# At most three sample gathers in flight in a deformable-convolution and mixture-of-experts kernel

## The chip, the core and the metric

The kernel runs on one core of one Trainium2 chip. The metric is the device time of one execution in microseconds (us); the time of a kernel is the median of its runs. The core has five engines that run their own instruction streams: TensorE (PE in the profile; its weight loads are listed as PEld), VectorE (DVE), ScalarE (ACT), GpSimd (POOL) and SyncE (SP). DMAs are issued by GpSimd and SyncE here, each through a queue of its own, and move data on the core's 16 DMA engines.

## The reference

The input `x` is 4 images of 256 channels and 64 x 64 pixels, in float32. First comes a residual branch: a normalisation over the channels and three modulated deformable 3 x 3 convolutions, each followed by a ReLU:

```
om   = conv3x3(x, w_off) + b_off              # 27 channels: 9 x (dy, dx) and 9 masks
ys   = gy + base_y + dy ;  xs = gx + base_x + dx
sampled = bilinear(x, ys, xs) * sigmoid(mask) # 9 samples of 256 channels for each pixel
out  = einsum('bikhw,oik->bohw', sampled, w) + b
```

A bilinear sample mixes four neighbouring pixels; outside the image they are zero. The branch's result is added to `x`. Then every pixel is a token of 256 features: a second residual branch normalises it, picks the two likeliest of 8 experts from a softmax gate, and adds the experts' outputs, weighted by their probabilities. An expert is 256 to 512, GELU, 512 to 256.

## The kernel before

**Stages and blocks.** A stage is one convolution layer of one image; `run` lists the 12 of them in `self.stages`, images interleaved so that the next layer of one image can be prepared beside another image's. A stage has 8 blocks of 512 pixels (`NB`, `BLK`), a block has 4 groups of 128 pixels (`TPB`) and 9 taps (`K`). `main_block` runs over the taps and, for each, over pairs of pixel groups: 36 gathers for a block, 288 for a stage, 3456 in all.

**The tables.** Each layer's input lies in HBM as a table (`tab`) in which a row holds a pixel's 256 channels and those of the pixel below it, so that two neighbouring rows, 4 KB, hold the four corners of a sample. `enter` writes the table through SyncE's queue. The offsets' convolution (line 357) and some VectorE work give, for each block, the row numbers `idx` and the mixing coefficients `cf`.

**One sample group.** `samples` issues an indirect DMA from GpSimd (line 503): 128 rows of 4 KB, 512 KB in all, into a buffer `g` of 128 x 1024 elements. VectorE then mixes the upper and lower corners (line 509) and the left and right ones (line 514), which gives `s`, 128 x 256, and ends the use of `g`. ScalarE multiplies with the mask (line 517). `turn`, which runs two pairs behind (`LAG = 2`), transposes a pair of samples on TensorE (line 532), ScalarE copies the result to SBUF (line 535), and when a tap's four groups are there `finish` multiplies the tap before it with its weights (line 555: four products of 128 x 128 by 128 x 512 into `acc`).

**Buffers and queues.** There are 10 buffers `g` (`GB = 10`) and 8 buffers `s`, so that VectorE can be some way ahead of TensorE. A gather waits until VectorE's line 514 has let go of the buffer that it takes. The DMAs of GpSimd's queue share eight landing semaphores in turn, so a DMA also waits until the eighth one in front of it on that queue has landed.

**The work beside it.** Around the gathers, in the same streams, stand the expert layers: for each of 163 expert steps `fetch` issues from GpSimd one weight gather (line 800, 128 rows of 9.2 KB) and two token gathers (line 812, 128 x 256); TensorE does lines 840, 856 and 874. `combine_fetch` (line 915) gathers the experts' results back, 256 times. A planner (`Lane`, `pump`) puts these pieces between the taps at a pace for each image. They begin when the first image has its third layer, after 2250 us, and are densest towards the end, where the last image's layers run beside them. GpSimd's queue is served in order: what stands behind a waiting gather waits with it.

Of the kernel before, what the change touches and what calls it, by code (L numbers as in the profile page):

```python
# [35 lines left out]
FT = 1 << FT_LOG  # L36
FU = FT // P
GB = 10
LAG = 2
LEAST = 2.0**-30  # L40
WINN = CC * (RPB + 2) * W
# [41 lines left out]
class Group:  # L83


    def __init__(self, b, n0, n1):
        self.b, self.n0, self.n1 = b, n0, n1
        self.nm = f"{b}_{n0}"
        self.M = (n1 - n0) * TPB

        self.NF = 2 * self.M * P // FT + E - 1


        self.half = (self.NF + 1) // 2
        self.zt, self.acc, self.gy, self.sums, self.py = {}, [], [], [], None
        self.order = [s // 2 + s % 2 * self.half for s in range(self.NF)]
# [21 lines left out]
class Weave:  # L118
# [3 lines left out]
    def __init__(self, ctx, tc, ins, out):  # L122
        nc = self.nc = tc.nc
        self.tc = tc
        self.ins = ins
        self.x = ins["x"].rearrange("b (c p) h w -> b p c (h w)", p=P)
        self.out_v = out.rearrange("b (c p) h w -> b p c (h w)", p=P)
        self.B = self.x.shape[0]

        def pool(name, bufs, **kw):  # L130
            return ctx.enter_context(tc.tile_pool(name=name, bufs=bufs, **kw))

        self.cst = pool("cst", 1)
        self.dram = pool("dram", 1, space=bass.MemoryType.DRAM)
        self.wkp = pool("wkp", 1)
        self.plan = pool("plan", 19)
        self.win = pool("win", 3)
        self.wt = pool("wt", 2)
        self.small = pool("small", 1)
        self.big = pool("big", 2)  # L140
        self.ffn = pool("ffn", 2)
        self.rt = pool("rt", 1)
        self.rt2 = pool("rt2", 2)
        self.gyp = pool("gyp", 4)
        self.smT = pool("smT", 2)
        self.smp = pool("smp", 8)
        self.gat = pool("gat", GB)
        self.ps = pool("ps", 3, space=bass.MemoryType.PSUM)
        self.ps1 = pool("ps1", 1, space=bass.MemoryType.PSUM)

        self.routes, self.tiles, self.sums = Lane(), Lane(), Lane()
        self.side, self.plans_side = [], []
        self.last = self.gathered = self.turned = None
        self.starting, self.draining, self.later = True, False, []
        self.pend, self.pairs = None, []

# [323 lines left out]
    def main_block(self, i, n, wins):  # L482
        l, b = self.stages[i]
        plan = self.plans.pop((l, b, n))
        for k in range(K):
            for t0 in range(0, TPB, 2):
                ss = self.samples(i, n, k, t0, plan)
                self.pairs.append((i, n, k, t0, wins, ss))
                if len(self.pairs) > LAG:
                    self.turn()  # L490
# [3 lines left out]
    def samples(self, i, n, k, t0, plan):  # L494


        nc = self.nc
        idx, cf = plan
        ss = []
        for t in (t0, t0 + 1):  # L500
            j = t * K + k
            g = self.gat.tile([P, 2, 2, C], F32, tag="g", name=f"g_{i}_{n}_{j}")
            self.gathered = nc.gpsimd.indirect_dma_start(  # L503
                out=g.rearrange("p x s f -> p (x s f)"),
                out_offset=None,
                in_=self.table(*self.stages[i]),
                in_offset=bass.IndirectOffsetOnAxis(ap=idx[:, j : j + 1], axis=0),
            )
            nc.vector.scalar_tensor_tensor(  # L509
                g[:, :, 0, :], g[:, :, 1, :], cf[:, j, 0:1], g[:, :, 0, :],  # L510
                ALU.mult, ALU.add,
            )
            s = self.smp.tile([P, C], F32, tag="s", name=f"s_{i}_{n}_{j}")
            self.last = nc.vector.scalar_tensor_tensor(  # L514
                s, g[:, 1, 0, :], cf[:, j, 1:2], g[:, 0, 0, :], ALU.mult, ALU.add
            )
            nc.scalar.activation(s, s, AF.Copy, scale=cf[:, j, 2:3])  # L517
            ss.append(s)
        return ss

    def turn(self):


        nc = self.nc
        i, n, k, t0, wins, ss = self.pairs.pop(0)
        nm = f"{i}_{n}_{k}"
        if t0 == 0:
            self.sT = self.smT.tile([P, CC, BLK], F32, tag="sT", name=f"sT_{nm}")
        tp = self.ps.tile([P, CC, 2 * P], F32, tag="tp", name=f"tp_{nm}_{t0}")
        for u in range(2):  # L530
            for c in range(CC):
                self.turned = nc.tensor.transpose(  # L532
                    tp[:, c, u * P : (u + 1) * P], ss[u][:, c * P : (c + 1) * P], self.ident
                )
        nc.scalar.copy(self.sT[:, :, t0 * P : (t0 + 2) * P], tp)  # L535
        if t0 + 2 == TPB:

            self.finish()
            self.pend = (i, n, k, self.sT, wins)
# [596 lines left out]
```

## Time and profile before

| | |
|---|---|
| median of 9 runs | 7514.78 us (7485.77 to 7528.69) |
| the profiled execution's own time | 7461.21 us |
| its span, first to last instruction | 7459.5 us |
| mean granted TensorE clock | 0.951 of full speed |
| bytes moved by DMA | 2223.73 MB, 298 GB/s on average |
| of these by GpSimd's queue (q0) | 1947.35 MB |
| gathers of line 503 | 3456, the first at 91.2 us, the last at 7007.0 us |
| GpSimd's time for one (writing its descriptors) | 939 / 975 / 3837 ns at least / median / at most |

Times in the profile count from the start of the span. An engine's busy time leaves out instructions that only wait or issue. A row of the timeline gives the start, the time taken, the engine, line and operation, and in brackets the idle time of the engine before it with what ended the wait; "issue" there means that the profile shows nothing that was waited for. For a GpSimd DMA the time taken is that of writing the descriptors; the data land later.

### The profile page before, as it was taken

The page shows a single profiled execution, that of the slowest core. Times are in us where ns is not written, and L with a number is a line of the kernel's source. Part 1 is how long each engine was busy: PE and PEld are TensorE (multiplying, and loading weights), DVE is VectorE, ACT ScalarE, POOL GpSimd, SP SyncE. Part 2 cuts the span into 40 slices and gives each one's busy share as a digit, 9 for nine tenths or more (in the row PEclk, how much of TensorE's full clock was granted, in tenths as well). Part 3 has the DMA queues.
Part 4 walks back from the last instruction along what each step waited for, and adds up shares of the span by engine and source line. Part 5 has one row for each costly group of instructions (what it writes and reads, how often), then busy time and mean ns, then how long its engine had stood idle before and what let it go on. Part 6 is the DMA issues. An engine that isn't in the chain of part 4 may idle for free.

```text
span 7459.5 us, 88985 instructions
## 1 busy us (share of the span) xinstructions
PE 6405.5 (86%) x26500; PEld 3594.1 (48%) x26500; DVE 4949.7 (66%) x11467; ACT 3263.0 (44%) x7141; POOL 4473.4 (60%) x4245
## 2 busy tenths in 40 slices
PE   7898888888898888889997888888888799978887
PEld 3443433334454444445554444444544455644665
DVE  6776777778997666667777656656768554667421
ACT  3444544445554444445453444444444343444322
POOL 4654666656666656556557656655656665666543
PEclk8999999999999999999998989999999999999988
DMA  8998999999999888888888888888888787888644
GB/s 270 338 326 277 355 339 339 350 339 354 365 355 320 303 303 297 291 316 320 316 309 302 300 278 316 303 294 297 316 306 299 253 275 248 289 303 289 212 139 124
DMA packets 800319, 2223.73 MB, mean 298 GB/s; under 512 B 104728, under 2 KB 302872, under 8 KB 794080
## 3 DMA queue, kind: packets, MB, share of 16 engines
q0 software_dynamic: 551200, 1947.35, 73.7%
q1 hardware_dynamic: 248640, 270.69, 10.9%
q8 instruction: 215, 3.52, 0.2%
q14 instruction: 264, 2.16, 0.1%
HBM read 2160.68 MB, written 196.40 MB: 316 GB/s over the span
## 4 chain that ended last, share of the span: by engine, by line
PE 68%; ACT 10%; issue 7%; another core or an unknown queue 6%; DVE 5%; DMA 2%; POOL 1%; SPq 0%; ACTq 0%; POOLq 0%; DVEq 0%
PE acc L555 34%; PE tp L532 10%; PE ph L856 7%; PE py L874 6%; PE po L357 6%; ACT sT L535 4%; ACT s L517 3%; DVE g L509 2%; DVE s L514 1%; PE pm L371 1%; ACT hT L866 1%; PE lp_tok L618 1%; PE ftp L840 1%; ACT win L577 1%
## 5 line engine op out<-in xcount | busy, mean ns | idle before, releaser
L503 POOL DMA_INDIRECT g<-tab,idx x3456 | 3686.0, 1067 | 2331.1 <-DVE s L514 1025.4
L555 PE MATMUL acc<-sT,wk 128*128 128x512 f32 x6912 | 3484.2, 619 | 259.5 <-ACT sT L535 151.2
L509 DVE SCALAR_TENSOR_TENSOR g<-g,cf 128x512 f32<-128x512 f32 x3456 | 2556.7, 742 | 262.4 <-DMA g<-tab,idx 246.6
L514 DVE SCALAR_TENSOR_TENSOR s<-g,cf 128x256 f32<-128x256 f32 x3456 | 1660.6, 482 | 1293.7 <-PE tp L532 701.1
L535 ACT COPY sT<-tp 128x512 f32<-128x512 f32 x1728 | 1002.1, 585 | 2303.3 <-PE tp L532 1534.0
L517 ACT ACTIVATE s<-s,cf 128x256 f32<-128x256 f32 x3456 | 1628.5, 508 | 241.3 <-DVE s L514 155.0
L555 PEld LDWEIGHTS acc<-sT,wk 128*128 128x128 f32 x6912 | 1193.0, 197 | 1110.5 <-issue 815.7
L532 PEld LDWEIGHTS tp<-ident,s 128*128 128x128 f32 x6912 | 889.7, 145 | 1640.9 <-issue 921.0
L532 PE MATMUL tp<-ident,s 128*128 128x128 f32 x6912 | 1278.0, 285 | 422.0 <-ACT s L517 220.9
L874 PE MATMUL py<-w,hT 128*128 128x256 f32 x2608 | 673.1, 396 | 109.5 <-ACT hT L866 64.0
L856 PE MATMUL ph<-fzT,w 128*128 128x256 f32 x2608 | 697.4, 401 | 64.1 <-ACT fzT L844 27.6
L874 PEld LDWEIGHTS py<-w,hT 128*128 128x128 f32 x2608 | 482.7, 195 | 250.8 <-ACT hT L866 100.9
L856 PEld LDWEIGHTS ph<-fzT,w 128*128 128x128 f32 x2608 | 492.4, 200 | 196.4 <-issue 67.4
L866 ACT ACTIVATE hT<-ph,w 128x256 f32<-128x256 f32 x652 | 281.9, 471 | 603.7 <-PE ph L856 353.8
L812 POOL DMA_INDIRECT zt<-z,tok x326 | 333.4, 1023 | 163.8 <-issue 88.3
L800 POOL DMA_INDIRECT w<-in_W,wrow x163 | 177.5, 1089 | 365.2 <-issue 126.7
L357 PE MATMUL po<-win,wo 128*32 128x504 f32 (+1 forms) x2304 | 365.0, 610 | 6.4 <-ACT win L301 2.1
L892 DVE TENSOR_TENSOR y<-py,w 128x512 f32<-128x512 f32 x163 | 111.7, 686 | 337.6 <-PE py L874 277.0
L915 POOL DMA_INDIRECT gy<-ys,slots x256 | 252.8, 988 | 105.0 <-issue 71.8
L930 DVE SCALAR_TENSOR_TENSOR ta<-gy,cw,ta 128x256 f32<-128x256 f32 x256 | 120.4, 479 | 127.2 <-DMA gy<-ys,slots 76.0
L357 PE MATMUL po<-win_pre,wo 128*32 128x504 f32 (+1 forms) x1152 | 184.9, 620 | 2.0 <-ACT om L366 2.0
L366 ACT ACTIVATE om<-po,bo 128x512 f32<-128x512 f32 x96 | 66.0, 687 | 257.4 <-PE po L357 164.5
(154 smaller groups left out, 2958.0 us busy)
## 6 DMA issues: line engine op xcount, KB each, us to landing
tab<-hv SPq DMA_DIRECT2D x512, 128.0 KB
g<-tab,idx POOLq DMA_INDIRECT x3456
ys<-y SPq DMA_DIRECT2D x163, 256.0 KB
tab<-h_pre SPq DMA_DIRECT2D x128, 256.0 KB
wk<-in_conv_w SPq DMA_DIRECT2D x99, 256.0 KB
xc_pre<-in_x SPq DMA_DIRECT2D x32, 512.0 KB
xr_tok<-in_x SPq DMA_DIRECT2D x32, 512.0 KB
t<-t_tok SPq DMA_DIRECT2D x32, 512.0 KB
```

Source lines behind the costliest of these rows:

```text
L357: nc.tensor.matmul(po[g * Q : (g + 1) * Q, :].rearrange("q (r w) -> q r w", w=W)[:, :, x0:x1], lhsT=self.wo[l][:, 3 * ky + kx, c, :], rhs= ...
L503: self.gathered = nc.gpsimd.indirect_dma_start(out=g.rearrange("p x s f -> p (x s f)"), out_offset=None, in_=self.table(*self.stages[i]), ...
L509: nc.vector.scalar_tensor_tensor(g[:, :, 0, :], g[:, :, 1, :], cf[:, j, 0:1], g[:, :, 0, :], ALU.mult, ALU.add,)
L514: self.last = nc.vector.scalar_tensor_tensor(s, g[:, 1, 0, :], cf[:, j, 1:2], g[:, 0, 0, :], ALU.mult, ALU.add)
L517: nc.scalar.activation(s, s, AF.Copy, scale=cf[:, j, 2:3])
L532: self.turned = nc.tensor.transpose(tp[:, c, u * P : (u + 1) * P], ss[u][:, c * P : (c + 1) * P], self.ident)
L535: nc.scalar.copy(self.sT[:, :, t0 * P : (t0 + 2) * P], tp)
L555: nc.tensor.matmul(acc[:, o, :], lhsT=self.wk[k][:, c, o * P : (o + 1) * P], rhs=sT[:, c, :], start=(k == 0 and c == 0), stop=(k == K - 1 ...
L812: self.nc.gpsimd.indirect_dma_start(out=zt, out_offset=None, in_=grp.zd, in_offset=bass.IndirectOffsetOnAxis(ap=grp.tok[:, j : j + 1], axi ...
L856: nc.tensor.matmul(ph[:, h, :], lhsT=w1[:, o : o + P], rhs=zT[:, c, :], start=(c == 0), stop=(c == CC - 1),)
L866: nc.scalar.activation(ht[:, h, :], ph[:, h, :], AF.Gelu, bias=w1[:, k : k + 1])
L874: nc.tensor.matmul(py[:, u, :], lhsT=hT[h // 2][:, h % 2, u * P : (u + 1) * P], rhs=w2[:, h * C : (h + 1) * C], start=(h == 0), stop=(h == ...
```

## The change

After issuing a sample gather, the kernel hands it to a new method `land`. That keeps the gathers that were issued last, and makes each one depend on the landing of the third sample gather in front of it. GpSimd waits for this before it issues the gather, so at most three sample gathers are in flight at any time. Weight, token and combine gathers are not counted and get no such wait. Buffers and their number stay as they are.

```diff
 GB = 10
+FLY = 3
 LAG = 2
...
         self.pend, self.pairs = None, []
+        self.flying = []
...
                 in_offset=bass.IndirectOffsetOnAxis(ap=idx[:, j : j + 1], axis=0),
             )
+            self.land(self.gathered)
             nc.vector.scalar_tensor_tensor(
...
+    def land(self, gather):
+
+        self.flying.append(gather.ins)
+        if len(self.flying) > FLY:
+            self.tc.add_manual_dep(
+                gather.ins,
+                self.flying.pop(0).name,
+                mybir.DependencyInfo(mybir.DependencyClass.Sync, mybir.DependencyReason.DATA),
+                reason="landed",
+            )
```

## The prediction

> **What bounds the kernel now.** I read the page first, then who waits for whom, then the line-503 gathers by stretches of time, and last two pieces of the timeline. From the page:
>
> ```profile
> span 7459.5 us, 88985 instructions
> PE 6405.5 (86%) x26500; PEld 3594.1 (48%) x26500; DVE 4949.7 (66%) x11467; ACT 3263.0 (44%) x7141; POOL 4473.4 (60%) x4245
> ...
> q0 software_dynamic: 551200, 1947.35, 73.7%
> ...
> PE 68%; ACT 10%; issue 7%; another core or an unknown queue 6%; DVE 5%; DMA 2%; POOL 1%; SPq 0%; ACTq 0%; POOLq 0%; DVEq 0%
> ```
>
> TensorE carries 68% of the chain that ended last; DMA is on it with 2%. So the gathers are early enough today, although their queue (q0) keeps the 16 DMA engines busy for 73.7% of the span. The waits say the same:
>
> ```profile
> POOL g L503 <- DVE s L514: 1025.4, 629, 15.6
> ...
> DVE g L509 <- DMA g<-tab,idx: 246.6, 88, 11.0
> ```
>
> GpSimd waits 1025.4 us for a free gather buffer, VectorE only 246.6 us for data, in 88 of 3456 gathers, and 229.4 us of that lies between 5750 and 7000 us. The question is whether a supply limited to three in flight is still faster than what is asked for. What is asked for, by stretches (columns: stretch, its length, GpSimd time and number of gathers, granted clock, DMA share, GB/s):
>
> ```profile
> 750.00:1000.00 250.00, 168.69 (x159) 0.99 0.96 353
> 3500.00:3750.00 250.00, 129.74 (x124) 0.97 0.88 314
> 6000.00:6250.00 250.00, 90.71 (x94) 0.97 0.78 265
> ```
>
> That is one gather in 1.57 us in the densest stretch, before the first expert; 2.02 us in the middle, where expert layers run beside the convolution; 2.66 us near the end. Inside a dense stretch the pace is steadier still and shorter, from the timeline of GpSimd:
>
> ```profile
> 1411.03 1.21 POOL L503 DMA_INDIRECT g<-tab,idx  x1 [0.48 <-DVE s L514]
> ...
> 1416.96 1.21 POOL L503 DMA_INDIRECT g<-tab,idx  x1 [0.58 <-issue]
> ```
>
> Four gathers per 5.93 us (one tap of a block), or 1.48 us each. How long one takes shows where GpSimd had been held up and VectorE has nothing left:
>
> ```profile
> 6029.79 0.95 POOL L503 DMA_INDIRECT g<-tab,idx  x1 [0.30 <-issue]
> 6031.04 0.95 POOL L503 DMA_INDIRECT g<-tab,idx  x1 [0.30 <-issue]
> 6032.29 0.94 POOL L503 DMA_INDIRECT g<-tab,idx  x1 [0.30 <-issue]
> ...
> 6033.95 0.75 DVE L509 SCALAR_TENSOR_TENSOR g<-g,cf 128x512 f32<-128x512 f32 x1 [5.94 <-DMA g<-tab,idx]
> ...
> 6036.43 0.75 DVE L509 SCALAR_TENSOR_TENSOR g<-g,cf 128x512 f32<-128x512 f32 x1 [1.11 <-DMA g<-tab,idx]
> ...
> 6038.60 0.75 DVE L509 SCALAR_TENSOR_TENSOR g<-g,cf 128x512 f32<-128x512 f32 x1 [0.80 <-issue]
> ```
>
> From issue to use: 4.16 us for the first, 5.39 for the one behind it, 6.31 for the third. GpSimd can issue every 1.25 us (0.95 and 0.30 before it), so a burst now has more than three under way.
>
> **The change, part by part.** Nothing is removed or moved: in the built program each engine has the same instructions in the same order. What differs is what gathers wait for. Before, each waited for its buffer (freed by line 514 of the tenth in front) and for its landing semaphore to be free again, the eighth DMA in front on GpSimd's queue. Now nearly all wait for the third gather in front. The weight, token and combine fetches (lines 800, 812, 915) stand in the same queue: they add no wait, but a gather that waits holds them up.
>
> *How often it waits.* The trace has part of the sixteen semaphore increments that end each DMA; I take the last one recorded before that semaphore's next DMA as the landing. Then 2325 of 3443 gathers are issued today before the third in front has landed, 1.82 us too early on average. So the wait is the rule.
>
> *The price of a loop of three.* When GpSimd only waits for landings, three gathers go out per latency: the period is (0.30 + L)/3, with 0.30 us the gap before each issue. L by how many other gathers were in flight at issue, from those with nearly complete records: none 4.46 us (21 gathers), one 5.16 (40), two 5.77 (188; 10% under 4.78, 10% over 6.89), three 6.27 (450). The wait lets a gather go when two are in flight. The 55 of the two-in-flight rows that keep their distance (over 1.5 us behind the one in front, 1.7 us before the next), as the loop would space them, have a median of 5.52 and a mean of 5.72. I take 5.55, nearer the median because the long ones are those beside other traffic, which the slices get back in part: (0.30 + 5.55)/3 = **1.95 us per gather**. Bounds: with the 13 gathers of the "one" row that keep the same distances, mean 4.95, it is 1.75 us; with the 94 of the "three" row, mean 6.09, it is 2.13 us.
>
> The page "DMA: Bandwidth & Descriptors" of the Trainium skill, section "Anatomy of one DMA — SWDGE (gpsimd) path", fits 2.0 us plus bytes over 436 GB/s: 3.2 us for this 512 KB gather. A loop of three would turn in 1.17 us by it, under the 1.25 us between two issues, and the change would cost nothing. The trace's lone gather already took 4.16 us, so I don't use it.
>
> *Stretch by stretch.* Ten gather buffers and eight sample buffers even out some 30 us, no more, so I compare demand and supply in slices of 250 us, and count only slices that run over.
> - 91 to 250 us: 95 gathers x 1.95 = 185 against 159: +26.
> - 250 to 2250 us: slices of 138, 121, 159, 148, 157, 143, 148, 147 gathers; x 1.95 less 250, the second (236) at nothing: 19 + 60 + 39 + 56 + 29 + 39 + 37 = +279. TensorE cannot hide it: it has the work of 1.48 us per gather and then waits.
> - 2250 to 5750 us: 1718 gathers and 78 weight fetches, each with two token fetches. These three hold GpSimd for 4.1 us (4617.90 to 4622.02 in the timeline), in which the loop of 1.95 misses about 2.2 us: 78 x 2.2 / 1718 = 0.10 per gather, so 2.05. Slices of 134, 123, 127, 122, 121, 124, 115, 117, 107, 129, 121, 124, 131, 127 give 25 + 2 + 10 + 0 + 0 + 4 + 0 + 0 + 0 + 14 + 0 + 4 + 19 + 10 = +88. Slices under 122 hide it, as now, behind expert products.
> - 5750 to 7010 us: 488 gathers, 49 weight fetches. GpSimd is held by the weight buffer, then sends about ten gathers at once, and VectorE is already waiting. In the burst shown the fourth would go 0.7 us later, the fifth 1.9, the sixth 2.9; their uses stand 6 to 10 us after issue, so most is absorbed. I take 1 us per burst, +50 (bounds 0 and 2.9 x 49 = 142).
>
> Sum: 26 + 279 + 88 + 50 = 443 us. The profiled execution took 7461.21 us, so 7904; the median of the runs is 0.72% above that execution, so 7904 x 1.0072 = **7960 us**. TensorE's work is not longer. Transfers on the SP queue may gain from the emptier queue, but nothing on the chain waits for them, so that counts for nothing.
>
> **The rivals.**
> - *The loop is quicker than its rows.* Fewer gathers also disturb each other less. At 1.75 us the same sum gives 7 + 78 + 0 + 20 = 105: 7620. For it: the rows come from a queue that is 93% busy. Against: the 55 well-spaced ones took 5.52 at the median all the same. Range of this case 1.60 to 1.85 us: 7535 to 7750.
> - *The loop is slower*, because the SP queue's packets and the weight fetches (1.2 MB) lie inside it. At 2.13 us: 43 + 473 + 351 + 100 = 967: 8490. For it: one in ten of the two-in-flight gathers took over 6.89 us. Against: the mean is 5.77.
> - *Faster: data come sooner.* Gather packets of 4096 B take 183 ns on average against 159 at the least; if crowding makes that difference, three in flight could land in the lone gather's 4.46 us. Then the period is 1.59 us, the sum above is 3, and weight and combine fetches find a shorter queue: at most VectorE's 246.6 us behind gathers and 76.0 behind combine fetches are to be had, and I would take a fifth, 7450. It decides from L below about 4.5 us. Against: with only one other in flight L is already 5.16.
> - *It does nothing.* If landings nearly always preceded the issue, 7515. Against: 2325 of 3443.
>
> **How the numbers follow.** The likeliest, 1.85 to 2.05 us per gather, spans 7750 to 8240: 0.55. Quicker loop 0.20, slower loop 0.14, faster 0.07, nothing 0.04. For 8 in 10 I leave out faster, nothing, the quickest quarter of the quicker loop and the worst part of the slower one: 7600 to 8380. This kernel's measurement can tell about 0.2% (15 us). Faster 0.07; same 0.05 (nothing, and the quick end of the quicker loop); slower 0.88.
>
> **What the next profile would show.** Right: gathers wait mostly for a gather's landing, over 1500 us in all; in the dense stretches about 128 per 250 us; the DMA share there falls from 0.95 to under 0.85; VectorE's wait for gathered data rises from 246.6 to some 600 us or more, and DMA and POOL appear on the chain; TensorE's busy time stays near 6400 us. Two in flight at issue and 5.55 us to landing confirm the loop. Wrong: dense stretches keep 157 per 250 us (the loop turns in under 1.6 us), or the slices from 2250 to 5750 grow more than the earlier ones (then it is the queue behind the wait, not the loop).

## The result, and the profile after

| | before | after |
|---|---|---|
| median | 7509.79 us, 31 runs (7472.95 to 7549.8) | 8382.19 us, 10 runs (8377.54 to 8399.98) |
| profiled execution | 7461.21 us | 8386.78 us |
| its mean granted TensorE clock | 0.951 | 0.923 |

The ratio is 1.1165 [1.1146, 1.1185]: the limit of three costs 872 us. The forecast was slower by 445 us; 8382 lies at the very end of the range, 2 us outside. The page of the changed kernel, with the lines that answer to those shown of before:

```profile
span 8385.1 us, 89077 instructions
PE 6849.9 (82%) x26500; PEld 3677.9 (44%) x26500; DVE 5153.7 (61%) x11467; ACT 3456.6 (41%) x7141; POOL 4224.6 (50%) x4245
...
q0 software_dynamic: 551200, 1947.35, 71.1%
...
DMA 19%; issue 6%; POOL 5%; PE 5%; DVE 3%; ACT 1%; another core or an unknown queue 0%; POOLq 0%; DVEq 0%; ACTq 0%; SPq 0%
```

DMA has taken TensorE's place on the chain of waits: 19% and 5%, where it was 2% and 68%. (The walk back along this chain breaks off at 5152 us, so its shares add up to some 40% only and tell of the last 3230 us; 18 of DMA's 19% are sample gathers.) GpSimd's busy time did not grow; it fell from 4473.4 to 4224.6 us. So the engine that issues the gathers did not run out of time, it stood still. The waits, with total, number of times and longest:

```profile
POOL g L505 <- DMA g<-tab,idx: 2408.8, 1572, 6.3
DVE g L512 <- DMA g<-tab,idx: 2385.5, 2101, 10.5
...
POOL g L505 <- issue: 652.2, 1269, 4.7
...
POOL g L505 <- DVE s L517: 90.8, 59, 5.6
```

The lines have moved by two and three: 505 is the gather (503 before), 512 and 517 VectorE's mixing (509 and 514). GpSimd's wait for a free buffer fell from 1025.4 to 90.8 us, and a wait for landings of 2408.8 us took its place. VectorE's wait for data went from 88 times to 2101. The gathers by stretches (columns as before):

```profile
750.00:1000.00 250.00, 116.54 (x124) 0.92 0.83 271
3500.00:3750.00 250.00, 112.76 (x116) 0.95 0.83 270
6000.00:6250.00 250.00, 107.03 (x109) 0.89 0.81 265
```

The dense stretch shows it best: 124 gathers where there were 159, and the DMA engines 83% busy, not 96%. The kernel is limited by supply while its DMA engines have room. (Stretches of one and the same clock time hold different work once one kernel is behind the other; so from here on the same gathers are compared, by their place in GpSimd's order, which the change leaves as it was.)

| the gathers that before had from | number | us each, before | after | difference, us |
|---|---|---|---|---|
| 91 to 250 us | 95 | | | +39 |
| 250 to 2250 us | 1156 | 1.730 | 2.127 | +459 |
| 2250 to 5750 us | 1718 | 2.038 | 2.267 | +393 |
| 5750 to 7010 us | 487 | 2.579 | 2.673 | +46 |
| the end, from the last gather's start | | 452 in all | 440 in all | -13 |

This adds up to +924; the first gather starts 1.5 us later, and the spans differ by 925.6 us. Why one gather takes 2.127 us and not 1.95 stands in GpSimd's timeline of the changed kernel:

```profile
1411.14 0.95 POOL L505 DMA_INDIRECT g<-tab,idx  x1 [0.35 <-issue]
1413.28 0.95 POOL L505 DMA_INDIRECT g<-tab,idx  x1 [1.19 <-DMA g<-tab,idx]
1415.84 0.95 POOL L505 DMA_INDIRECT g<-tab,idx  x1 [1.61 <-DMA g<-tab,idx]
1417.31 0.95 POOL L505 DMA_INDIRECT g<-tab,idx  x1 [0.52 <-issue]
```

By the trace's semaphore records the gathers third in front of these landed at 1410.40, 1412.54, 1415.10 and 1416.57 us. Each gather begins 0.74 us after the landing that it waited for. GpSimd takes the wait in an instruction of its own, which begins 0.024 us after the landing and takes 0.017 us; the gather starts 0.715 us after its beginning. The prediction put 0.30 us there. The two rows marked "issue" had waited for a landing too: the idle time of 0.52 us is shorter than the 0.74 us after the landing, so that the view finds nothing to blame. Of the 652.2 us under "issue", part is therefore the same cause.

### The profile page after: what moved, and what is told of

The parts are those of the page before. It is cut to its first block, busy times and chain, and to the rows that moved or that the text cites. A ratio compares the mean times of both kernels' runs of the same rounds, so it can differ in the third digit from the quotient of the medians.

```text
span 8385.1 us, 89077 instructions
## 1 busy us (share of the span) xinstructions
PE 6849.9 (82%) x26500; PEld 3677.9 (44%) x26500; DVE 5153.7 (61%) x11467; ACT 3456.6 (41%) x7141; POOL 4224.6 (50%) x4245
## 5 line engine op out<-in xcount | busy, mean ns | idle before, releaser
L505 POOL DMA_INDIRECT g<-tab,idx x3456 | 3424.1, 991 | 3701.9 <-DMA g<-tab,idx 2408.8
L512 DVE SCALAR_TENSOR_TENSOR g<-g,cf 128x512 f32<-128x512 f32 x3456 | 2583.4, 748 | 2434.0 <-DMA g<-tab,idx 2385.5
L569 PE MATMUL acc<-sT,wk 128*128 128x512 f32 x6912 | 3618.5, 639 | 151.3 <-ACT sT L549 129.8
L520 ACT ACTIVATE s<-s,cf 128x256 f32<-128x256 f32 x3456 | 1738.3, 508 | 2846.7 <-DVE s L517 2519.0
L546 PE MATMUL tp<-ident,s 128*128 128x128 f32 x6912 | 1397.8, 300 | 986.8 <-ACT s L520 851.7
L546 PEld LDWEIGHTS tp<-ident,s 128*128 128x128 f32 x6912 | 863.1, 150 | 2472.5 <-ACT s L520 1718.8
L569 PEld LDWEIGHTS acc<-sT,wk 128*128 128x128 f32 x6912 | 1246.2, 205 | 1053.7 <-issue 763.5
L870 PE MATMUL ph<-fzT,w 128*128 128x256 f32 x2608 | 739.8, 419 | 62.1 <-ACT fzT L858 39.4
L870 PEld LDWEIGHTS ph<-fzT,w 128*128 128x128 f32 x2608 | 516.4, 210 | 203.3 <-ACT fzT L858 69.1
L359 PEld LDWEIGHTS po<-win,wo 128*32 128x32 f32 x2304 | 76.4, 115 | 204.6 <-issue 165.9
```

The lines of the kernel that those rows point to most:

```text
L359: nc.tensor.matmul(po[g * Q : (g + 1) * Q, :].rearrange("q (r w) -> q r w", w=W)[:, :, x0:x1], lhsT=self.wo[l][:, 3 * ky + kx, c, :], rhs= ...
L505: self.gathered = nc.gpsimd.indirect_dma_start(out=g.rearrange("p x s f -> p (x s f)"), out_offset=None, in_=self.table(*self.stages[i]), ...
L512: nc.vector.scalar_tensor_tensor(g[:, :, 0, :], g[:, :, 1, :], cf[:, j, 0:1], g[:, :, 0, :], ALU.mult, ALU.add,)
L546: self.turned = nc.tensor.transpose(tp[:, c, u * P : (u + 1) * P], ss[u][:, c * P : (c + 1) * P], self.ident)
L569: nc.tensor.matmul(acc[:, o, :], lhsT=self.wk[k][:, c, o * P : (o + 1) * P], rhs=sT[:, c, :], start=(k == 0 and c == 0), stop=(k == K - 1 ...
L870: nc.tensor.matmul(ph[:, h, :], lhsT=w1[:, o : o + P], rhs=zT[:, c, :], start=(c == 0), stop=(c == CC - 1),)
```

## The experiments

Two things are told apart here. Is the loop itself the price, that is (gap + L)/N for N in flight, or is it what stands behind the waiting gather in GpSimd's queue? And is the 0.74 us an avoidable cost of waiting in a separate instruction, or the gather's own way from a satisfied wait to its first descriptor? The kernels ran on several chips: the kernel before takes 6806 us on two of them and 7507 to 7513 us on others, so a time is compared only with times from the same chip.

### The size of the limit: two, four, five

```diff
-FLY = 3
+FLY = 2
```

and likewise with 4 and 5.

> The limit at two. The latency with one other in flight was 4.95 to 5.2 us before. Theory 1: period (0.74 + 5.05)/2 = 2.90 us, everywhere the bound; 3456 x 2.90 = 10020, 0.14 more for 2205 gathers beside experts = 310, and 530 us ahead of the first and behind the last gather: about 10,860 us. With a gap of 0.30 us: 2.68 us, 10,100 us.

> The limit at four. The latency with three others in flight was 6.1 to 6.3 us before. Theory 1 (gap 0.74 us): period (0.74 + 6.1)/4 = 1.71 us, and the sum by slices gives about +100: 7610 us. With a gap of 0.30 us: 1.60 us, +50 at most: 7515 to 7560. Theory 2, any wait for a landing costs by what it holds up in the queue: well above 7700.

> The limit at five. Period by theory 1 (0.74 + 6.5)/5 = 1.45 us, under the 1.48 us of the densest stretch: 7510 us, no difference to the kernel before beyond 0.3%. By theory 2 (queue held up): 7600 or more. If fewer gathers in the queue help the other transfers, it would show here as less than 7495.

On the chip where the kernel before takes 6806 us: 10558.9 us for two (1.5514 [1.5487, 1.5541]), 7224.99 for four (1.0614 [1.0598, 1.0629]), 6841.24 for five (1.0055 [1.0043, 1.0067]). The expected times were worked out for a chip with 7510 us, so the differences are what can be compared. Four cost 419 us, not some 100: in the first 1152 gathers the loop took 1.78 us and not 1.71, and the kernel before takes 1.62 us there on this chip, where it took 1.73 in the first profile. Five cost 0.55%, not under 0.3%. Two came out between the sum with a gap of 0.74 us (10,860) and the one with 0.30 (10,100), mostly because a gather had landed 4.76 us after its start (0.95 + 3.81), not 5.05. The loop in parts, from the first 1152 gathers; the three parts are taken from those that waited for a landing:

| limit | landing to start | descriptors | descriptors to landing | sum / limit | us per gather, all |
|---|---|---|---|---|---|
| 2 | 0.74 | 0.95 | 3.81 | 2.75 | 2.79 |
| 3 | 0.74 | 0.97 | 4.53 | 2.08 | 2.13 |
| 4 | 0.74 | 0.99 | 5.11 | 1.71 | 1.78 |
| 5 | 0.74 | 1.04 | 5.67 | 1.49 | 1.63 |

The gap is 0.74 us whatever the limit, and the sum over the limit gives the pace. With 0.30 us in its place the sums would be 2.53, 1.93 and 1.60 for two to four, about 0.2 us under what was measured for each. With five, 44% of these gathers wait for a landing, and the pace is nearly the kernel before's own there, 1.623 us. (With two, the scheduler also moved some instructions; the loop decides all the same.) The groups of GpSimd's gathers say how the wait fades; after the bar stand busy time, mean ns, and idle time by what ended it:

With two in flight:

```profile
L505 POOL DMA_INDIRECT g<-tab,idx x3456 | 3372.9, 976 | 5977.9 <-DMA g<-tab,idx 5017.0 <-issue 500.5 <-DMA tab<-h_pre 57.2
```

With four:

```profile
L505 POOL DMA_INDIRECT g<-tab,idx x3456 | 3501.6, 1013 | 2438.2 <-DMA g<-tab,idx 1184.0 <-issue 576.9 <-DVE s L517 126.9
```

With five:

```profile
L505 POOL DMA_INDIRECT g<-tab,idx x3456 | 3615.2, 1046 | 1897.4 <-issue 545.8 <-DVE s L517 457.3 <-DVE g L512 235.5
```

From two to five, the wait for landings falls from 5017.0 us to 192.9, and the one for buffers that VectorE's line 517 lets go of (457.3 us) is now larger: for most gathers the loop is no longer what ends last.

### The wait in the gather itself

Apart from its landing, a gather waits for its buffer. In this kernel every fourth gather also waits for the sample seventh in front, which frees the buffers of the three behind it as well; these have the landing as their only wait, and it sits in the gather instruction.

```diff
             self.land(self.gathered)
+            self.free_ahead(self.gathered)
...
+        if k % 4 == 0 and k >= 7:
+            self.tc.add_manual_dep(
+                gather.ins,
+                self.sampled[k - 7].name,
...
```

> Still three gathers in flight, but only every fourth gather waits for VectorE (for the sample seven in front of it, which frees the buffers of the next three too); the other three have the landing as their only wait. Theory 1, the time between a landing and the next issue was mis-sized (0.74 us in the changed kernel's trace against 0.30 in the sum, because a landing is waited for in an instruction of its own ahead of the gather): where the landing is the gather's own and only wait, the gap falls to some 0.27 us, on average to 0.39, the period from 2.09 to 1.97 us, and the same sum (2.11 per gather where experts run) gives 7510 + 545 = 8055 us. Theory 2, the gap does not matter, the loop is held by the DMA itself (it would take 6.1 us per turn anyway) or by what stands behind the waiting gather in GpSimd's queue: 8380 us, unchanged.

It ran a second time beside the changed and the unchanged kernel.

> Three in flight, three of four gathers with the landing as their only wait, on the same chip as the changed kernel. Theory A, latency does not depend on the gap: the mean gap of gathers that wait for landings falls from 0.74 to 0.44 us, 0.10 us per gather, about 300 us under the changed kernel. Theory B, a shorter gap brings more overlap of transfers and the latency takes most of it back: 5.75 instead of 5.50 us, 0.02 to 0.05 us per gather, 70 to 150 us under the changed kernel.

> The changed kernel once more, so that it stands on one chip beside the others of this call. Its own bound, three gathers per 0.74 + 5.5 us, has nothing of the chip's TensorE pace in it, so its time should stay near 8380 us even where the kernel before takes 6806; if the loss were a fixed price per wait instead, it would be 6806 + 870 = 7680.

> The kernel before with a profile, on the same chip. If this chip gives 6806 us again, its profile should show where the 700 us against the first profile are: in TensorE's clock (0.978 against 0.951 explains only 2.8%), or in gathers that land sooner (L under 6.2 us), or in shorter waits between engines.

Measured: 8282.29 us, then 8284.85 (8281.02 to 8289.17); the changed kernel on the same chip 8374.01 (8373.08 to 8380.33); the kernel before 6809.22. That the changed kernel takes 8374 us on this quicker chip too was expected of a loop; a fixed price per wait would have made it 7680. The first expectation for the new kernel, 8055 or 8380 us, was missed on both sides. Saved are 89 us, in the range of theory B (70 to 150 us) and not the 300 us of theory A. From start to landing a gather now takes 5.72 us for 5.50, also near B's 5.75, but not for B's reason: the way from written descriptors to landing stayed (4.55 us for 4.53). The timeline of the second run shows where the time went:

```profile
1411.22 1.34 POOL L506 DMA_INDIRECT g<-tab,idx  x1 [2.38 <-DMA g<-tab,idx]
1414.27 1.34 POOL L506 DMA_INDIRECT g<-tab,idx  x1 [1.71 <-DMA g<-tab,idx]
1416.03 0.94 POOL L506 DMA_INDIRECT g<-tab,idx  x1 [0.42 <-issue]
```

The first two have the landing as their own wait: they start 0.26 us after it (landings at 1410.96 and 1414.01) but take 1.34 us, and not 0.95. The third still waits in a separate instruction and starts 0.74 us after its landing (1415.29). From landing to written descriptors it is 1.60 us in the one way and 1.68 to 1.71 in the other; the time has gone into the instruction. Per gather 0.029 us was saved (2.097 for 2.126), and 3456 x 0.029 = 100 us against 89 measured. (The scheduler also moved a few instructions.) So the gap became 0.26 us and the loop stayed: a turn with 0.30 us in place of 0.74 and all else as it was could not be made.

### A memset that takes the wait

Here a one-column memset on GpSimd, ahead of each gather, carries the wait for the landing.

```diff
+            self.land(nc.gpsimd.memset(self.idle[:, :PAD], 0.0))
...
-            self.land(self.gathered)
+            self.flying.append(self.gathered.ins)
...
-        if len(self.flying) > FLY:
+        if len(self.flying) >= FLY:
             self.tc.add_manual_dep(
-                gather.ins,
+                first.ins,
```

> Three in flight, and ahead of each gather GpSimd sets one column of a spare tile to zero; this small instruction, not the gather, waits for the landing. If the turn is the time from a landing to written descriptors plus a rest of 4.53 us that does not react, every 0.1 us more on that way costs 0.033 us per gather, some 105 us in all. One more instruction behind the landing should make the way 1.9 to 2.3 us instead of 1.71: 8570 to 9000 us. If the rest shortens as the way gets longer (the DMA engines hold the loop), the time stays within 60 us of 8378.

> The changed kernel on the chip of this call, as the base for the one with the added instruction: 8370 to 8390 us on any chip.

Measured 8424.92 us (8401.56 to 8427.25) beside 8387.93 for the changed kernel: +37 us, not the hundreds expected. The time lies within 60 us of 8378, which had been named for a rest that shortens as the way gets longer; but the way did not get longer, so that this run can't tell the two apart. The memset was meant to lengthen the gap by its own start, and it did not:

```profile
1413.21 0.10 POOL L507 MEMSET idle<- 128x1 f32 x1 [0.86 <-DMA g<-tab,idx]
1413.87 0.94 POOL L508 DMA_INDIRECT g<-tab,idx  x1 [0.56 <-DVE g L515]
1416.19 0.10 POOL L507 MEMSET idle<- 128x1 f32 x1 [1.38 <-DMA g<-tab,idx]
1416.85 0.94 POOL L508 DMA_INDIRECT g<-tab,idx  x1 [0.56 <-DVE g L515]
```

The landings were at 1413.095 and 1416.080. The memset begins 0.11 us later, the gather 0.66 us after the memset's start, though the memset takes 0.10 us. So some 0.7 us lie ahead of the first descriptor that begin when the wait is over, beside the memset, and from landing to start it is 0.77 us. Per gather that is a third of 0.03 us more: 0.03 / 3 x 3456 = 35 us, against 37 measured. The miss of the expectation is one more sign that this time belongs to the gather. It also agrees with the loop's rate: what a gather's turn grows by, the kernel pays a third of, 3456 times. By itself this is weak, since one of the four times is 8401.56 us.

### The limit in one half of the kernel only

The index `i` counts the stages: the first four run before the expert layers begin.

```diff
-            self.land(self.gathered)
+            if i < 4:
+                self.land(self.gathered)
```

and, for the other half, `i >= 4`.

> The limit only in the first four stages (1152 gathers, no experts beside them). Those take 2.12 us each in the changed kernel, so 2440 us in all, whatever the chip: on a chip where the kernel before takes 7510 us this is +460 to +490 us, on one with 6806 us some +570 (there its 1152 gathers take at most 1.63 us each). If the later stages give back what the early ones lose, or the loss needs the experts in the queue, it is much less, under +200.

> The limit only from the fifth stage on (2304 gathers, experts beside most of them). If the loss lies in each stretch by itself, the two parts add up to the whole: 8374 less 7373 (the limit in the first four stages alone) over 6806 gives 7807 us. If a part of the loss comes only from the whole being late, it is under 7700.

The early half alone costs 568 us (7373.03 beside 6805.5; 1.0839 [1.0818, 1.0859]), as expected. The late half alone, on a chip where the kernel before takes 7506.67 us, costs 430 us (7936.72; 1.0575 [1.0559, 1.0591]). The 7807 us expected are 1001 us over the 6806 of the quicker chip, and can't be held against the 430 us here, where the kernel before is slower. What can be compared is the same gathers. The limit of the late kernel begins with gather 1153. Its gathers 1153 to 2969 (up to 5750 us in the kernel before) take 430 us longer than in the first profile of the kernel before and those behind them 45 us, in the changed kernel 431 and 46; its first 1152 take 1994 us beside 1987. In the early kernel, on the quicker chip, the first 1152 take 2443 us, beside 2450 in the changed kernel there, and the others 4403 us, beside 4412 in the kernel before there. So each half pays its own loss, and nothing that one loses is paid back in the other. The stretches of the early kernel:

```profile
750.00:1000.00 250.00, 116.90 (x124) 0.92 0.82 272
4000.00:4250.00 250.00, 147.02 (x130) 1.00 0.91 326
```

And of the late one:

```profile
750.00:1000.00 250.00, 169.41 (x159) 0.99 0.95 353
4000.00:4250.00 250.00, 117.05 (x111) 0.96 0.85 278
```

With the limit 124 and 111 gathers in 250 us, without it 159 and 130 (124 and 130 on the quicker chip, 159 and 111 on the other). The cost sits where the limit is.

### Gathers of half the size

Gathers of 2 KB rows, which leave out part of the samples, with and without the limit, to see what the limit costs when data land sooner.

```diff
-                out=g.rearrange("p x s f -> p (x s f)"),
+                out=g[:, 0].rearrange("p s f -> p (s f)"),
```

> Three in flight, but each gather brings rows of 2 KB (one table row instead of two, 256 KB in all); the mix is made of what is there, so a part of the samples is left out; VectorE's operations keep their sizes. Theory 1, a turn is 1.71 us from a landing to written descriptors plus 4.53 us, of which only the transfer itself (8 packets of 159 ns on each DMA engine, 1.27 us) shrinks, to 0.64: turn 5.6 us, 1.87 us per gather and 0.05 to 0.2 for the gathers that come late to the loop, about 7550 us. Theory 2, the loop is held by bytes (DMA share 0.83): the time falls to the kernel without a limit, 6800 us. Theory 3, only fixed latency: 8370 us.

> The same gathers of 2 KB rows without a limit: the floor of the comparison with three in flight and 2 KB rows. TensorE carries the chain of the kernel before, so 6700 to 6800 us.

Measured 7917.56 us with the limit and 7838.82 without (the kernel before: 7506.67). Neither was expected: with the limit it was to be about 7550, 6800 or 8370 us, without it 6700 to 6800. The scheduler put VectorE's operations in another order (for one, line 514 four times in a row), and GpSimd waits longer for buffers than in the kernel before. Without the limit:

```profile
POOL g L503 <- DVE s L514: 1427.1, 817, 13.6
```

So these two compare with each other only. The limit costs 79 us, 1%, where with full gathers it costs 11.65%. With the limit:

```profile
POOL g L505 <- DVE s L517: 1129.4, 709, 10.8
...
POOL g L505 <- DMA g<-tab,idx: 416.1, 360, 4.8
```

The turn of the loop is about 0.74 + 1.06 + 2.63 = 4.43 us, a third of it 1.48 us, and some 29% of the first 1152 gathers wait for it; these 1152 take 1.86 us each, and buffers are the larger wait (1129.4 against 416.1 us). The same limit is dear or cheap by whether its turn, over N, is longer than the pace that the engines behind it ask for.

### Six and seven

The expert layers and the gathers as they are, with `FLY = 6` and `FLY = 7`.

> The limit at six. Gap 0.74, descriptors 1.04 and some 6.0 us after them make (7.8)/6 = 1.30 us per gather, below what is asked for anywhere on average: 6806 us, within 0.3%. With the limit at five it was 35 us more; if that was not the loop but a price of the waits themselves, it stays at +35 here.

> The limit at six, a second time. It was 0.5% faster than the kernel before on a chip where that takes 7507 us. If the emptier queue really helps, it is 0.3 to 0.7% faster again; if it was that chip or chance, it is within 0.2% or slower, the more so where the kernel before takes 6806 us and asks for gathers faster.

> The limit at seven; the landing semaphores alone already hold the queue at eight DMAs. No cost from the loop ((0.74 + 1.05 + 6.3)/7 = 1.16 us). If the limit at six is faster because fewer gathers are queued, this lies between it and the kernel before: 0 to 0.4% faster.

Six: 7472.73 us, 0.9953 [0.994, 0.9967], and again 7485.04 us, 0.9966 [0.9947, 0.9984]. Seven: 7499.68, 0.9988 [0.997, 1.0005]. The first of the two for six was expected within 0.3% of the kernel before, or 35 us slower if the waits have a price of their own, and is neither; the second is as expected if the gain is not chance, and so is seven. A limit of six is 0.3 to 0.5% faster than no limit on chips where the kernel before takes 7.51 ms; with seven no difference can be told. Where the 28 to 34 us come from is not settled. The limit of six holds hardly any gather: in its two traces 4 of 944 and 5 of 952 gathers with full landing records start 0.74 us after the landing of the sixth in front, and in the first profile of the kernel before only 20 of 3456 were issued with six or more others in flight. Six was not tried on the chip where the kernel before takes 6806 us and a limit of five already costs 0.55%.

## Why the prediction was wrong in size

**What held.** The mechanism and the side were right: TensorE bound before, then a loop of three by landings. L was right: 5.50 us (0.97 + 4.53) for 5.55. So was the sum over slices. (The prediction has the same instructions on each engine; the trace has 92 more, all of them semaphore instructions on GpSimd, 3672 for 3580. The rest stands as it did.) With 2.13 us per gather the prediction itself has 43 + 473 + 351 for the first three parts, and with its 50 for the last 917 us; measured were 39, 459, 393 and 46. The first two parts and the last are within 14 us.

**The step that failed** is the gap in "(0.30 + L)/3, with 0.30 us the gap before each issue". The 0.30 us came from gathers issued one behind the other with nothing to wait for. That it would also hold behind a wait was assumed, not read from a row. Behind a wait that has just ended it is 0.74 us, and from landing to written descriptors 1.71 us instead of 1.25. A period of 1.95 us became 2.127, in these terms: the gap of loop-bound gathers +0.44 / 3 = +0.147; L -0.05 / 3 = -0.017; and a gap of 0.88 us over all gathers, with the 5% that something else held up, +0.14 / 3 = +0.047. That is +0.177, the whole difference (the 0.88 us is what 3 x 2.127 leaves beside L, so the sum closes by its making; the 0.74 us is read from the trace). By the prediction's own slices it is worth 473 - 279 between 250 and 2250 us and 351 - 88 up to 5750, 457 us together: with the shorter period six of the later slices counted nothing, and with the longer one most of them run over.

The hint stood in the rows shown of before: the gather at 1411.03, issued behind a wait for VectorE, took 1.21 us to write its descriptors, while those behind an idle 0.30 us took 0.94 and 0.95. A wait that ends costs something at this instruction, and a loop that waits every time pays it every time.

**A smaller miss.** What the expert fetches add to the loop was put at 0.10 us per gather between 2250 and 5750 us; 2.267 less 2.127 is 0.14. Over 1718 gathers that is at most 69 us, and 42 of them can be seen (393 for 351).

**The rivals.** The slower loop, with chance 0.14, had the size (2.13 us per gather, 8490 us) but for a reason that did not hold: L is not longer for other queues' packets, the gap is. The quicker loop and the faster case needed an L well under 5.5 us. Data do land sooner with fewer in flight, 4.53 us after the descriptors with three and 3.81 with two, but not soon enough: by the table of limits each one fewer shortens the way by 0.56 to 0.72 us, while the turn is shared by one gather less. Nor did the packets of 4096 B get shorter with three in flight: on GpSimd's queue they took 200 ns on average, beside 183 before. "It does nothing" asked for landings ahead of the issue; GpSimd waited for them 1572 times.

**What the next profile would show.** Landing waits over 1500 us: 2408.8. Dense slices of about 128 gathers: 119 to 124 between 750 and 2000 us. DMA share there from 0.95 to under 0.85: 0.83 to 0.85. VectorE's wait for data some 600 us or more: 2385.5, far more, since it now waits at three gathers of five. DMA and POOL on the chain: 19% and 5%. Two in flight at issue: 3075 of 3456. The middle stretch did not grow more than the earlier ones (393 us in 3500, 459 in 2000), so by the prediction's own sign the queue behind the wait is not the cause; the early kernel, which loses 568 us with no expert fetch beside its limit, says the same. Wrong was TensorE's busy time, put "near 6400 us": it is 6849.9, with as many instructions. The group of the convolution's products in the changed kernel:

```profile
L569 PE MATMUL acc<-sT,wk 128*128 128x512 f32 x6912 | 3618.5, 639 | 151.3 <-ACT sT L549 129.8
```

Before, one took 619 ns. The mean granted clock fell from 0.951 to 0.923, which is about the 3% that one product got longer. The busy time grew by 7%; the durations of all matmuls added up one by one grew by 3.7% only, so they overlap less in the profile, and why is not settled. TensorE did not make the kernel slower: in the loop's stretches 95% of the gathers wait for a landing.

**The skill's rule.** The page "DMA: Bandwidth & Descriptors", section "Anatomy of one DMA — SWDGE (gpsimd) path", gave an estimate of 3.2 us for this gather and so no cost. The turn is 0.74 + 0.97 + 4.53 = 6.24 us. The measurement decides, and the forecast was right not to use it. The same section calls the making of descriptors small; here it takes 0.95 to 0.97 us of the turn.

## What to carry to other kernels

A limit of N transfers in flight has a pace of its own, the whole turn over N: from a landing to the next start, the writing of descriptors, and the way to the next landing. Compare it with the pace that the engines behind ask for, stretch by stretch, and take each of its terms from rows in which an instruction really came out of a wait, since the gap between two instructions that wait for nothing is shorter. A first limit to try is the smallest whose pace is clearly under the demand: here six gains up to half a per cent on the slower chips; on the quicker ones five costs half a per cent and four 6%; three costs 12 to 23% by the chip.

## What the runs showed of the hardware that was not expected

- A gather on GpSimd's queue starts 0.74 us after the landing that it waited for in a separate instruction, at every limit from two to five. With the wait in the gather itself it starts after 0.26 us and then writes its descriptors for 1.34 us, not 0.95. A memset of 0.10 us between the two delays the gather by 0.03 us only.
- The way of a gather from written descriptors to landing grows with the number in flight: 3.81, 4.53, 5.11 and 5.67 us for limits of two to five. Halving the rows at a limit of three took it from 4.53 to 2.63 us, three times the 0.64 us that the shorter packets were expected to save.
- The mean granted TensorE clock rose together with TensorE's busy share in these runs: 0.865 at 72% (limit of two), 0.923 at 82% (three), 0.963 at 88% (four), 0.975 at 91% (five), 0.977 at 92% (none); two, four and five ran on one chip, none on another of the quicker ones. The kernel before on a slower chip has 0.951 at 86%.
- One kernel, two kinds of chip: the kernel before takes 6806 us on two of them and about 7510 us on others, while the changed kernel takes 8374 to 8388 us wherever it ran. The page of the kernel before on the quicker chip:

```profile
span 6807.5 us, 88985 instructions
PE 6229.4 (92%) x26500; PEld 3527.9 (52%) x26500; DVE 4963.9 (73%) x11467; ACT 3278.5 (48%) x7141; POOL 4436.8 (65%) x4245
...
PE 73%; ACT 8%; DVE 6%; DMA 5%; issue 4%; POOL 3%; SPq 0%; ACTq 0%; DVEq 0%; POOLq 0%
```

TensorE is busy 176 us less there, as its clock of 0.977 for 0.951 would make it; the rest of the 652 us between the two spans lies in TensorE's idle time. Gathers do not land sooner there: from start to landing they take 7.0 us on average, beside 6.4. But the first profile has 44 pauses of the matmuls of over 2 us (162 us in all, the longest 10.2) for which it shows nothing that was waited for, and the quicker chip's has none. Why is open. A kernel that is bound by the supply of gathers does not show the difference, so the same limit costs 12% on one chip and 23% on another.
